# Two block products of the last projection taken as quarter products, and a division moved by one product

## The chip, the core and the metric

The kernel runs on one core of a Trainium2 chip. The core has a matrix engine (TensorE, PE in the profile; its weight loads are shown apart as PEld), three engines for elementwise work (VectorE = DVE, ScalarE = ACT, GpSimd = POOL) and SyncE (SP), which here issues almost all DMAs. Each engine works through its own list of instructions; semaphores tie the lists together. Matmul results are accumulated in PSUM banks; everything else lies in SBUF, the on-chip memory. The metric is the device time of one execution in microseconds (us); lower is better.

## What is computed

Two layers, one after the other, on a batch of 8 images of 512 channels and 32x32 = 1024 positions, in float32. Each layer is a group norm, an attention with 8 heads of 64 channels over the 1024 positions, an output projection with a bias, and the addition of the layer's input:

```python
xn = groupnorm(x) * gn_scale + gn_bias                        # x: (8, 512, 1024)
q, k, v = split(einsum('oc,bcn->bon', qkv_w, xn) + qkv_b, 3)
attn = softmax(einsum('bhdi,bhdj->bhij', q, k) / sqrt(64), axis=-1)
out = einsum('bhij,bhdj->bhdi', attn, v)                      # back to (8, 512, 1024)
x = einsum('oc,bcn->bon', proj_w, out) + proj_b + x
```

The two layers differ in the number of groups (8 and 32) and in the weights.

## The kernel before

**Units.** The work is cut into 16 units, one for each layer and image. A unit makes v, q and k (three products of a 512x512 weight with the 512x1024 normed input), then runs the attention in 64 steps (`attention`), each with a score matmul (line 953), an exponential on ScalarE (961), a sum on VectorE (998) and a product with v (981). The projection of a unit is worked in the following unit, between k and the attention. The last unit has no follower. Behind its attention stand therefore two projections: first that of the unit before (called here the earlier projection; `project`, line 700), then its own, the last one (`project_last`, line 833).

**Fewer products by recursion.** Every 512x512 times 512x1024 product is made as a 2x2 block product by a scheme that needs 7 block products in place of 8 (numbered 1 to 7, run in the order 1, 6, 2, 7, 5, 4, 3). It needs sums and differences of blocks. `Right` holds the right-hand side, the moving operand: `outer[k]` is the block for product k, and `mix(i)` makes one of the four differences on VectorE (line 221; `mix(0)` makes the block of product 5, `mix(1)` that of product 6 and reads the fourth pair of channels). One block product is 256x256 times 256x512. It can be done in two ways:

- as a *whole block product* (`steps` in `project_last`, matmuls at line 413): four matmuls of 128x512;
- as *quarter products*, by the same scheme once more: seven *parts*, each one matmul of 128x256 (line 448). `single(k, rooms, engine, kept)` (line 241) gives the four subtractions of 128x256 which that needs and enters the seven operands in `inner[k]`.

**The stream.** `Stream.product` (line 415 on) issues quarter products so that the tail of one lies inside the next: part 1; then `close()`, which issues the tail of the product before it (parts 4 and 3, and its `finish`); then parts 6, 2, 7 and 5. The parts 1, 6 and 5 add up in one PSUM place, `one`. Between them ScalarE copies this running sum into the quarters of the result (`seed`, line 457: 11 after part 1, 21 after part 6, 12 after part 5, 22 after part 4), and it copies part 7 to an SBUF tile `late` (line 462), which is added on GpSimd later on (`add_late`, line 557). Part 5 may overwrite `one` only when seed 21 has read it. `finish` takes the result out of PSUM, for the most part on VectorE, and calls `hook("o", k)`, which runs what was hung on product k by `at("o", k, ...)`: at this place it enters the lists of the engines.

**What is hung on the earlier projection.** In the last unit the earlier projection carries the end of the last attention: the transposition and reduction of the row sums (`transposed`, `reduced`, at products 1 and 6), the first difference `mix(0)` (at product 2), `reciprocals` (at product 7) and, at product 3, the last of all, `divide` and two bias steps. `reciprocals` (line 1032) makes the reciprocals of the softmax sums on VectorE, stores them to DRAM (`drec`) and loads them back twice, 64 rows each, spread over the rows (`rb`). `divide` (line 1054, instruction at 1056) multiplies the last 128 channels (the fourth pair of channels, in `xn` for the last unit) by `rb` on VectorE, and `add_bias` (line 1061, instruction at 1063) adds the v bias on ScalarE in two halves.

**The last projection.** `project_last` makes all seven products as whole block products, in the order 1, 5, 6, 7, 2, 4, 3. Product 1 is begun with two matmuls ahead of the tail of the earlier projection. Its result goes to an SBUF tile `p1` with the bias by two activations on ScalarE (line 866); the sums of product 5 are added to two of the four result tiles `res` (in the space of q) on VectorE (line 872); GpSimd adds `p1`, `u2` and `u3` to the result tiles (`more`, line 853); VectorE finishes them, and SyncE stores them (line 858 and on). Here the PSUM places are named outright: `sbank[1]`, `apair[0]`, `sbank[0]`, `apair[1]` in turn.

Of the kernel before, what the change touches and what calls it, by code (L numbers as in the profile page):

```python
# [13 lines left out]
AF = mybir.ActivationFunctionType  # L14
ALU = mybir.AluOpType
# [8 lines left out]
GAMMA, BETA, QB, KB, VB, PB = range(6)  # L24
# [10 lines left out]
def fast_path(ctx, tc, x, qkv_wT, proj_wT, vecs, groups, out, flag):  # L35
# [5 lines left out]
    nc = tc.nc  # L41
# [7 lines left out]
    FD2 = FD // 2  # L49
# [7 lines left out]
    def pool(name, bufs, **kw):  # L57
# [53 lines left out]
    def raw(inst):  # L111
        return getattr(inst, "ins", inst)
# [7 lines left out]
    def follows(inst, other, reason):  # L120
        tc.add_manual_dep(raw(inst), name_of(other), DEP, reason=reason)
# [21 lines left out]
    def block_rows(t, r, h):  # L143
        return t[2 * r * P : 2 * (r + 1) * P, ts(h, FD)].rearrange("(i p) n -> p i n", p=P)
# [32 lines left out]
    def mix_left(left, engine=None):  # L177

        engine = engine or nc.vector
        add, sub = engine.tensor_add, engine.tensor_sub  # L180
        f = {k: left.block[:, k - 1, :] for k in range(1, 8)}
        a11, a21, a12, a22 = (left.block[:, :, i : i + P] for i in range(0, FD, P))
        s1, s2, s4 = (left.made[:, :, i : i + P] for i in range(0, 3 * P, P))
        return [
            partial(add, f[5], f[7], f[4]), partial(sub, f[6], f[5], f[1]),
            partial(sub, f[7], f[1], f[7]), partial(sub, f[3], f[2], f[6]),
        ], [
            partial(add, s1, a21, a22), partial(sub, s2, s1, a11),
            partial(sub, a21, a11, a21), partial(sub, s4, a12, s2),
        ]  # L190
# [220 lines left out]
    def run(steps):  # L411
        for step in steps:
            step()  # L413
# [135 lines left out]
    def in_two(cols):  # L549
        return cols.rearrange("p (a b) -> p a b", a=2)  # L550

    def twice(late):
        return late[:, None, :].to_broadcast([P, 2, FD2])

    def add_late(t, late):
        cols = in_two(t[:, 1, :])
        return nc.gpsimd.tensor_add(cols, cols, twice(late))  # L557
# [275 lines left out]
    def project_last(stream, w, left, again, res, rest):  # L833

        l, b = units[w.u]
        right = w.right_o
        add = nc.vector.tensor_add

        def steps(bank, k):
            return [  # L840
                partial(
                    nc.tensor.matmul, bank[:, i, :],
                    again[:, k - 1, :] if (c, i) == (0, 1) else left.outer(k)[:, c, ts(i, P)],
                    right.outer[k][:, c, :], start=c == 0, stop=c == 1, skip_group_check=True,
                )
                for i in range(2) for c in range(2)
            ]

        def sums(name):
            return accpool.tile([P, 2, FD], F32, tag="acc", name=f"{name}_last")  # L850

        def more(r, h, t, after=None):
            n = nc.gpsimd.tensor_add(res[r, h], res[r, h], t)
            if after is not None:
                follows(n, after, "one engine at a time on SBUF")

        def store(r, h):
            nc.sync.dma_start(block_rows(out[b], r, h), res[r, h])

        first = steps(sbank[1], 1)  # L860
        run(first[:2])
        stream.close()
        run(first[2:])
        p1 = sums("p1")
        for i in range(2):
            nc.scalar.activation(p1[:, i, :], sbank[1][:, i, :], AF.Identity, bias=vec[:, l, PB, i : i + 1])
        right.mix(1)
        run(steps(apair[0], 5))
        more(0, 0, p1, right.mix(3))
        for i in range(2):  # L870
            for t in (res[0, 1], res[1, 1]):
                add(t[:, i, :], apair[0][:, i, :], t[:, i, :])
        run(steps(sbank[0], 6))
        right.mix(2)
        u2 = sums("u2")
        add(u2, sbank[0], p1)
        more(0, 1, u2, rest())
        run(steps(apair[1], 7))
        u3 = sums("u3")
        for i in range(2):  # L880
            nc.vector.scalar_tensor_tensor(
                u3[:, i, :], apair[1][:, i, :], step_vec[:, l, PB, i : i + 1], u2[:, i, :], ALU.add, ALU.add
            )
        more(1, 1, u3)
        more(1, 0, u3)
        engines = mybir.EngineType
        tc.mark_branch_hint_location(
            GENERAL, "LikelyTaken", (engines.PE, engines.Activation, engines.DVE)
        )
        run(steps(sbank[1], 2))  # L890
        add(res[0, 0], sbank[1], res[0, 0])
        store(0, 0)
        store(1, 1)
        nc.tensor.matmul(apair[1][:1, 0, :1], both, ones[:, :1], start=True, stop=True)
        nc.scalar.copy(flag, apair[1][:1, 0, :1])
        run(steps(apair[0], 4))
        good = nc.values_load(flag[0:1, 0:1], min_val=0, max_val=P)
        add(res[1, 0], apair[0], res[1, 0])
        store(1, 0)

        rows, t = block_rows(out[b], 0, 1), res[0, 1]
        for step in steps(sbank[0], 3)[:2]:
            on("PE", step(), "s0", 0)  # L903
        on("DVE", add(t[:, 0, :], sbank[0][:, 0, :], t[:, 0, :]), "s0", 0)
        nc.sync.dma_start(rows[:, 0, :], t[:, 0, :])
        for h, bank in enumerate((sbank[0][:, 1], sbank[1][:, 1])):
            cols = ts(h, FD2)
            for c in range(2):
                n = nc.tensor.matmul(  # L909
                    bank[:, :FD2], left.outer(3)[:, 1, P:] if c else again[:, 2, :], right.outer[3][:, c, cols],  # L910
                    start=c == 0, stop=c == 1, skip_group_check=True,
                )
                on("PE", n, f"s{h}", 1)
            on("DVE", add(t[:, 1, cols], bank[:, :FD2], t[:, 1, cols]), f"s{h}", 1)  # L914
            nc.sync.dma_start(rows[:, 1, cols], t[:, 1, cols])
        return good

# [199 lines left out]
    first = {sel: mix_left(left) for sel, left in (("v", slot_v), ("q", slot_q), ("k", left_first_k))}  # L1117
# [11 lines left out]
    right = Right(xn, xt)  # L1129
# [13 lines left out]
    for u in range(2 * B):  # L1143
        w = Unit()
        w.u, w.right, w.last, w.ready, w.ao = u, right, {"v": []}, {}, ao
        w.v = vpool.tile([P, NT, C], F32, tag="v", name=f"v_{u}")
        l, _ = units[u]
# [3 lines left out]
        def at(sel, k, *parts):  # L1151
            hooks.setdefault((sel, k), []).extend(parts)
# [29 lines left out]
        def alone(t, row, i):  # L1182
            return t[:, row, i * FD2 : (i + 1) * FD2]

        def in_k(*which):
            return [alone(w.kp[r], row, i) for r, row, i in which]
# [96 lines left out]
        stream = Stream((u + 1) % 2)  # L1283
# [48 lines left out]
        right = Right(xn, xt) if not last else None  # L1332
        mixing = {}
        if not last:
# [5 lines left out]
            late = u == 0  # L1340
# [96 lines left out]
    both = const.tile([P, 1], F32, name="both")  # L1437
# [10 lines left out]
    at("o", 6, reduced, bias_2[1])  # L1448
    at("o", 2, partial(w.right_o.mix, 0))
    at("o", 7, reciprocals)  # L1450
    at("o", 3, divide, *bias)

    res = {(r, h): q_pairs[r][:, :, ts(h, FD)] for r in range(2) for h in range(2)}
    for (r, h), t in res.items():
# [266 lines left out]
```

## Time and profile before

| | us |
|---|---|
| median of 3 runs (3162.94 to 3163.63) | 3163.36 |
| the profiled execution, its own time | 3163.43 |
| its span, from the first to the last instruction | 3161.6 |

The mean granted clock of TensorE over the span is 0.999 of full speed. The stretches at the end (busy us of each engine, in brackets the instructions that are counted):

| stretch, us from the start | what runs | PE | DVE | ACT | POOL |
|---|---|---|---|---|---|
| 3059.0 to 3111.0 (52.0) | last half of the last attention | 52.00 (488) | 47.30 (51) | 34.45 (37) | 9.32 (9) |
| 3111.0 to 3131.4 (20.4) | earlier projection | 20.40 (98) | 18.56 (23) | 12.66 (35) | 13.35 (8) |
| 3131.4 to 3157.1 (25.7) | last projection | 25.66 (67) | 15.27 (22) | 3.55 (8) | 14.84 (7) |
| 3157.1 to 3161.6 (4.5) | last sum and stores | 0.00 | 0.42 (1) | 0.00 | 0.00 |

A float32 matmul is shown by the profile as two instructions. In the lines of the timeline each line is a group: its start, its length, the engine, the line of the kernel, the operation, output and inputs; in brackets stands the idle time ahead of it, and what ended it. In the chain of waits each line is a start, a length and what held up the end in that time.

### The profile page before, as it was taken

The numbers are of one execution on the slowest core, as the hardware profiler recorded it, in microseconds if no ns is written. First come the engines' busy times: TensorE is split into PE (matmuls) and PEld (weight loads), VectorE is DVE, ScalarE is ACT, GpSimd is POOL, SyncE is SP. The second block draws the span as 40 slices with busy tenths as digits, with TensorE's granted clock in tenths as the row PEclk, the third lists the DMA queues.
The fourth block names the chain that finished last, engine by engine and source line by source line (L and its number), as shares of the span: only waits on it lengthen the run. The fifth ranks groups of instructions, "written<-read, shape, count | busy, mean of one in ns | idle before, by whom it ended". The sixth has DMA issues, their size and how long they took to land.

```text
span 3161.6 us, 63820 instructions
## 1 busy us (share of the span) xinstructions
PE 3154.5 (100%) x24278; PEld 2030.4 (64%) x24278; DVE 2687.7 (85%) x3150; ACT 2039.9 (65%) x3573; POOL 1283.6 (41%) x982
## 2 busy tenths in 40 slices
PE   9999999999999999999999999999999999999999
PEld 8476584765847658475584756748567485674845
DVE  8988979889798897888979888798887988879787
ACT  3766767666676666766667666676666766667664
POOL 5245271542715426053361533615336162351514
PEclk9999999999999999999999999999999999999999
DMA  5333343443533324233142331423314333242302
GB/s 190 111 132 129 115 162 109 146 135 104 173 107 138 123 62 169 77 117 129 57 169 80 123 120 57 169 80 133 110 57 169 91 129 102 61 170 87 127 16 95
DMA packets 155923, 365.78 MB, mean 116 GB/s; under 512 B 30176, under 2 KB 46048, under 8 KB 155616
## 3 DMA queue, kind: packets, MB, share of 16 engines
q1 hardware_dynamic: 155040, 361.04, 34.3%
q8 instruction: 196, 3.21, 0.4%
q14 instruction: 111, 0.91, 0.1%
q10 hardware_dynamic: 576, 0.61, 0.1%
HBM read 299.72 MB, written 59.77 MB: 114 GB/s over the span
## 4 chain that ended last, share of the span: by engine, by line
PE 100%; DVE 0%; DMA 0%; ACT 0%; issue 0%; ACTq 0%
PE a L981 28%; PE s L953 27%; PE s L448 24%; PE a L448 18%; PE a L953 1%; PE a L413 1%; PE s L413 1%; PE s L348 0%; DMA xn<-x_dram 0%; DVE stats L273 0%; PE a L285 0%; PE s L909 0%; PE s L903 0%; PE s L285 0%; DVE q L914 0%
## 5 line engine op out<-in xcount | busy, mean ns | idle before, releaser
L961 ACT ACTIVATE p<-s 128x1024 f32<-128x1024 f32 x976 | 997.2, 1023 | 516.2 <-PE s L953 492.2
L981 PE MATMUL a<-p,v 64*64 64x512 f32 x8192 | 1101.0, 589 | 0.0
L953 PE MATMUL s<-q,k 64*64 64x512 f32 x7808 | 1059.2, 590 | 0.1
L998 DVE TENSOR_TENSOR acc<-acc,p 128x1024 f32<-128x1024 f32 x768 | 955.6, 1244 | 75.0 <-ACT p L961 31.6
L457 ACT COPY a<-s 128x256 f32<-128x256 f32 x1728 | 615.4, 358 | 346.9 <-PE s L448 247.0
L981 PEld LDWEIGHTS a<-p,v 64*64 64x64 f32 x8192 | 384.0, 131 | 495.3 <-ACT p L961 351.0
L953 PEld LDWEIGHTS s<-q,k 64*64 64x64 f32 x7808 | 385.4, 133 | 429.7 <-issue 429.2
L462 ACT COPY late<-s 128x256 f32<-128x256 f32 x432 | 161.0, 373 | 198.5 <-PE s L448 187.2
L448 PE MATMUL s<-k,w 128*128 128x256 f32 x672 | 195.0, 379 | 0.0
L998 DVE TENSOR_TENSOR acc<-p,p 128x1024 f32<-128x1024 f32 x128 | 156.0, 1219 | 10.0 <-ACT p L961 10.0
L1429 POOL TENSOR_TENSOR k<-xn 128x256 f32<-128x256 f32 x15 | 11.8, 787 | 369.3 <-PE s L953 260.5
L1013 DVE STREAM_TRANSPOSE tr<-acc 128x1024 f32<-128x1024 f32 x128 | 158.0, 1234 | 0.0
L1021 DVE TENSOR_REDUCE red<-tr 128x32 f32<-128x1024 f32 x128 | 154.1, 1204 | 0.0
L448 PE MATMUL a<-xn,w 128*128 128x256 f32 x492 | 146.4, 379 | 0.0
L448 PEld LDWEIGHTS s<-k,w 128*128 128x128 f32 x672 | 125.1, 190 | 18.0
L448 PE MATMUL a<-xt,w 128*128 128x256 f32 x456 | 135.7, 379 | 0.0
L305 POOL TENSOR_TENSOR y<-var,half 128x4 f32<-128x4 f32 (+1 forms) x17 | 19.7, 1157 | 277.2 <-DVE var L303 277.2
L557 POOL TENSOR_TENSOR q<-q,late 128x512 f32<-128x512 f32 x64 | 100.2, 1565 | 64.6 <-ACT a L457 45.5
L1008 DVE TENSOR_TENSOR ao<-a,tmp 128x512 f32<-128x512 f32 x120 | 82.4, 687 | 39.6 <-ACT tmp L1007 39.0
L448 PE MATMUL s<-xn,w 128*128 128x256 f32 x372 | 110.7, 379 | 0.0
L566 POOL TENSOR_TENSOR v<-v,late 128x512 f32<-128x512 f32 x60 | 89.8, 1496 | 48.8 <-DVE v L668 35.3
L448 PE MATMUL s<-xt,w 128*128 128x256 f32 x368 | 109.5, 379 | 0.0
(298 smaller groups left out, 5141.1 us busy)
## 6 DMA issues: line engine op xcount, KB each, us to landing
w<-iq SPq DMA_DIRECT2D x105, 448.0 KB, 3.5
w<-ik SPq DMA_DIRECT2D x105, 448.0 KB, 7.4
w<-io SPq DMA_DIRECT2D x105, 448.0 KB, 7.6
w<-iv SPq DMA_DIRECT2D x98, 448.0 KB, 3.7
rb<-drec SPq DMA_DIRECT2D x128, 256.0 KB, 3.9
res<-x_dram SPq DMA_DIRECT2D x32, 512.0 KB, 5.9
mid<-res SPq DMA_DIRECT2D x32, 512.0 KB, 2.8
xn<-mid SPq DMA_DIRECT2D x32, 512.0 KB, 3.6
```

The source lines that it names most:

```text
L448: nc.tensor.matmul(to, at, moving, start=start, stop=j != 1, skip_group_check=True),
L457: n = nc.scalar.copy(dst, one)
L462: on("ACT", nc.scalar.copy(late, seventh), s, 1)
L557: return nc.gpsimd.tensor_add(cols, cols, twice(late))
L566: return nc.gpsimd.tensor_add(cols, cols, parts)
L953: nc.tensor.matmul(bank[e * H : (e + 1) * H, j, :], w.k[pr][j * H : (j + 1) * H, t * P + e * H : t * P + (e + 1) * H], w.q[pr][j * H : (j ...
L961: exp = nc.scalar.activation(p, bank, AF.Exp, scale=SCALE)
L981: nc.tensor.matmul(banks[r][j * H : (j + 1) * H, :], w.v[rows, t, lo : lo + D], p[rows, j, :], start=(t == 0), stop=(t == NT - 1),)
L998: state["sums"].append(nc.vector.tensor_add(acc, state["first"] if t == 1 else acc, p))
L1008: i1 = nc.vector.tensor_add(w.ao[:, pr, ts(qh, FD)], banks[1], tmp)
L1013: nc.vector.transpose(tr, state["acc"].pop(c))
L1021: nc.vector.tensor_reduce(red[:, :, qh, :], state["tr"].rearrange("p j (f i) -> p j f i", i=BL), AX.X, ALU.add)
```

## The change

- Products 1 and 5 of the last projection become quarter products of the same stream that makes the earlier projection. `single` makes their operands: for product 1 four subtractions on GpSimd, put right ahead of the stream; for product 5 four subtractions on VectorE, hung on product 4 of the earlier projection behind the division. Their rooms are the eight 128x256 pieces of the first k pair.
- The division and its two bias steps are hung on product 4 of the earlier projection, where they were on product 3.
- `first` takes the result of product 1 out of PSUM (two activations on ScalarE, the late part added on GpSimd), `fifth` that of product 5 (four sums on VectorE, the late part added to two tiles on GpSimd).
- Product 6, still a whole block product, is begun with two matmuls ahead of the tail of product 5. The PSUM places of the products that follow are now taken by the stream's parity (`main`, `aux`, `other`, `spare_main`).

```diff
-        first = steps(sbank[1], 1)
-        run(first[:2])
+        def first(main, m, late):
+            for i in range(2):
+                n = nc.scalar.activation(
+                    p1[:, i, :], main[:, i, :], AF.Identity, bias=vec[:, l, PB, i : i + 1]
+                )
+                on("ACT", n, m, i)
+            add_late(p1, late)
+            more(0, 0, p1, mixed)
+
+        def fifth(main, m, late):
+            for i in range(2):
+                for t in (res[0, 1], res[1, 1]):
+                    on("DVE", add(t[:, i, :], main[:, i, :], t[:, i, :]), m, i)
+            for t in (res[0, 1], res[1, 1]):
+                add_late(t, late)
+
+
+        p1 = sums("p1")
+        stream.product(left.quarters(1), right.inner[1], False, first)
+        right.mix(1)
+        mixed = right.mix(3)
+        i = stream.n % 2
+        stream.product(left.quarters(5), right.inner[5], False, fifth)
+        (main, aux), (spare_main, other) = ((apair[j], sbank[1 - j]) for j in (i, 1 - i))
+        sixth = steps(other, 6)
+        run(sixth[:2])
         stream.close()
-        run(first[2:])
-        p1 = sums("p1")
-        for i in range(2):
-            nc.scalar.activation(p1[:, i, :], sbank[1][:, i, :], AF.Identity, bias=vec[:, l, PB, i : i + 1])
-        right.mix(1)
-        run(steps(apair[0], 5))
-        more(0, 0, p1, right.mix(3))
-        for i in range(2):
-            for t in (res[0, 1], res[1, 1]):
-                add(t[:, i, :], apair[0][:, i, :], t[:, i, :])
-        run(steps(sbank[0], 6))
+        run(sixth[2:])
         right.mix(2)
         u2 = sums("u2")
-        add(u2, sbank[0], p1)
+        add(u2, other, p1)
         more(0, 1, u2, rest())
-        run(steps(apair[1], 7))
+        run(steps(spare_main, 7))
...
-    at("o", 3, divide, *bias)
+    rooms = [alone(k_pairs[0], row, i) for row in range(2) for i in range(4)]
+    run(w.right_o.single(1, rooms[:3], nc.gpsimd, rooms[3]))
+    at("o", 4, divide, *bias, *w.right_o.single(5, rooms[4:7], nc.vector, rooms[7]))
```

What is left out renames PSUM places of the products 7, 2, 4 and 3. New line numbers: the sum of product 4 of the last projection stands at line 912 (898 before), the division at 1070, the bias at 1077, the subtractions of product 5 are shown at 1170 (the call in `hook`), the activations of `p1` at 862.

More of the change, by code (lines that the diff above doesn't have):

```diff
@@ L858, in store @@
             nc.sync.dma_start(block_rows(out[b], r, h), res[r, h])
-        first = steps(sbank[1], 1)
-        run(first[:2])
-        stream.close()
-        run(first[2:])
-        p1 = sums("p1")
-        for i in range(2):
-            nc.scalar.activation(p1[:, i, :], sbank[1][:, i, :], AF.Identity, bias=vec[:, l, PB, i : i + 1])
-        right.mix(1)
-        run(steps(apair[0], 5))
-        more(0, 0, p1, right.mix(3))
-        for i in range(2):
-            for t in (res[0, 1], res[1, 1]):
-                add(t[:, i, :], apair[0][:, i, :], t[:, i, :])
-        run(steps(sbank[0], 6))
+        def first(main, m, late):
[21 more added lines that the diff above has]
+        run(sixth[:2])
+        stream.close()
+        run(sixth[2:])
         right.mix(2)
         u2 = sums("u2")
-        add(u2, sbank[0], p1)
+        add(u2, other, p1)
         more(0, 1, u2, rest())
-        run(steps(apair[1], 7))
+        run(steps(spare_main, 7))
         u3 = sums("u3")
-        for i in range(2):
+        for r in range(2):
             nc.vector.scalar_tensor_tensor(
-                u3[:, i, :], apair[1][:, i, :], step_vec[:, l, PB, i : i + 1], u2[:, i, :], ALU.add, ALU.add
+                u3[:, r, :], spare_main[:, r, :], step_vec[:, l, PB, r : r + 1], u2[:, r, :], ALU.add, ALU.add
             )
@@ L889, in project_last @@
         )
-        run(steps(sbank[1], 2))
-        add(res[0, 0], sbank[1], res[0, 0])
+        run(steps(aux, 2))
+        add(res[0, 0], aux, res[0, 0])
         store(0, 0)
         store(1, 1)
-        nc.tensor.matmul(apair[1][:1, 0, :1], both, ones[:, :1], start=True, stop=True)
-        nc.scalar.copy(flag, apair[1][:1, 0, :1])
-        run(steps(apair[0], 4))
+        nc.tensor.matmul(spare_main[:1, 0, :1], both, ones[:, :1], start=True, stop=True)
+        nc.scalar.copy(flag, spare_main[:1, 0, :1])
+        run(steps(main, 4))
         good = nc.values_load(flag[0:1, 0:1], min_val=0, max_val=P)
-        add(res[1, 0], apair[0], res[1, 0])
+        add(res[1, 0], main, res[1, 0])
         store(1, 0)
         rows, t = block_rows(out[b], 0, 1), res[0, 1]
-        for step in steps(sbank[0], 3)[:2]:
-            on("PE", step(), "s0", 0)
-        on("DVE", add(t[:, 0, :], sbank[0][:, 0, :], t[:, 0, :]), "s0", 0)
+        for step in steps(other, 3)[:2]:
+            on("PE", step(), f"s{i}", 0)
+        on("DVE", add(t[:, 0, :], other[:, 0, :], t[:, 0, :]), f"s{i}", 0)
         nc.sync.dma_start(rows[:, 0, :], t[:, 0, :])
-        for h, bank in enumerate((sbank[0][:, 1], sbank[1][:, 1])):
-            cols = ts(h, FD2)
+        for h, bank in enumerate((other[:, 1], aux[:, 1])):
+            cols, name = ts(h, FD2), f"s{(i + h) % 2}"
             for c in range(2):
@@ L912, in project_last @@
                 )
-                on("PE", n, f"s{h}", 1)
-            on("DVE", add(t[:, 1, cols], bank[:, :FD2], t[:, 1, cols]), f"s{h}", 1)
+                on("PE", n, name, 1)
+            on("DVE", add(t[:, 1, cols], bank[:, :FD2], t[:, 1, cols]), name, 1)
             nc.sync.dma_start(rows[:, 1, cols], t[:, 1, cols])
```

## The prediction

> **What bounds the kernel now.** I read the page first: one engine fills the span.
>
> ```profile
> PE 3154.5 (100%) x24278; PEld 2030.4 (64%) x24278; DVE 2687.7 (85%) x3150; ACT 2039.9 (65%) x3573; POOL 1283.6 (41%) x982
> ...
> PE 100%; DVE 0%; DMA 0%; ACT 0%; issue 0%; ACTq 0%
> ```
>
> So time is won only by taking matmuls away, and lost by any instruction that makes TensorE (PE) wait. The change touches the last 50 us, so next I read the chain of waits there (start, length, what):
>
> ```profile
> 3130.71 0.86 PE s L448 x4
> 3131.57 1.72 PE s L413 x4
> ...
> 3135.87 3.43 PE a L413 x8
> 3139.30 3.69 PE s L413 x8
> ```
>
> A part of a quarter product (L448) takes 0.43 us; a 128x512 step of a whole block product (L413) 0.86 us, four of them 3.43 us. The sixth product took 3.69: 0.26 us of waiting, for the chain division, bias, mix. In all, PE waits for nothing else from 3128 on, and the last product ends at 3157.07. The timeline shows what stands around it (start, length, engine and line, output and inputs; in brackets the wait ahead):
>
> ```profile
> 3128.53 1.12 SPq L1049 DMA_DIRECT2D rb<-drec  x2
> ...
> 3130.32 0.36 ACT L457 COPY a<-s 128x256 f32<-128x256 f32 x1 [0.45 <-PE s L448]
> ...
> 3131.16 2.35 POOL L723 TENSOR_TENSOR spare<-spare,u_o 128x1024 f32<-128x1024 f32 x1
> ...
> 3135.39 1.22 DVE L1056 SCALAR_TENSOR_TENSOR xn<-xn,rb 128x1024 f32<-128x1024 f32 x1
> ...
> 3136.65 1.33 ACT L1063 ACTIVATE xn<-xn,vec 128x512 f32<-128x512 f32 x2 [2.48 <-DVE xn L1056]
> 3137.89 1.24 ACT L866 ACTIVATE p_last<-s,vec 128x512 f32<-128x512 f32 x2
> ```
>
> Two things are to be seen. The division (L1056) needs `rb`, whose two loads were only issued at 3128.53 and 3129.06. And the copy at 3130.32 is the seed that an L448 matmul at 3130.98 (part 5 of the earlier projection's third product) waits for. When `rb` is there, the DMA view tells (first issue alone, then the tile's own row):
>
> ```profile
> rb<-drec SPq DMA_DIRECT2D x1, 256.0 KB, 3.5
> ...
> DMA to landing us min/median/max: 3.5/3.7/3.9
> ```
>
> The first landed at 3128.53+3.5 = 3132.0, the second at 3129.06+3.9 = 3133.0. The load needs the reciprocals (3126.54) by way of `drec` (3127.11); nothing ahead of that is moved.
>
> [...] L866's input was ready at 3135.87, but it stood behind L1063, which waited 2.48 us for the division, and began at 3137.89. [...] L557 takes 1.27 us alone and took 2.18 beside the division; the mix at 3122.06 took 2.36 in place of 1.22 behind an L723, and the next L557 then waited for it. [...] the granted clock (third figure from the right in these stretches) after the last matmul ended at 3157.07, and in the start of the kernel:
>
> ```profile
> 8.50:9.00 0.50, 0.47 (x5) 0.47 (x6) 0.15 (x2) 0.00 (x0) 0.00 (x0) 0.76 0.99 336
> 9.00:12.00 3.00, 3.00 (x15) 3.00 (x16) 2.83 (x11) 0.85 (x2) 0.71 (x1) 0.50 1.03 350
> ...
> 3159.25:3159.50 0.25, 0.00 (x0) 0.00 (x0) 0.00 (x0) 0.00 (x0) 0.00 (x0) 0.53 0.06 16
> ```
>
> The clock fell 2.2 us after the last matmul; at the start it was low for some 3.4 us of steady work.
>
> **The change part by part.**
>
> *Fewer matmuls.* Products 1 and 5 go from 4 steps of 0.86 to 7 parts of 0.43: 3.45-3.02, twice, is **-0.86 us** of PE. The sixth's wait of 0.26 goes too, since its mix is then early: **-0.26**.
>
> *Four subtractions on GpSimd ahead of the stream* (128x256, 0.73 each by the L1384 rows). They read `xn` pairs 0 and 1 and write the room of the first k pair, which the scores have left. They start when L1384 ends, 3102.9[...]. Taken in turn, the VectorE queue is about 2.5 us late at 3109; it idles 1.85 us before the copy at 3111.15 and 0.62 before L578, so the `rb` chain does not move: 0 (at most +0.5).
>
> *The division, its two bias steps and four new subtractions, at product 4 instead of 3.* No DMA among them, and nothing on SP changes place. In the instruction order of the changed kernel, VectorE has division and subtractions ahead of product 3's L719; ScalarE has the **two bias steps ahead of the seed copy of product 3** that was at 3130.32, with everything of the stream behind it. So:
> - the division could start at 3133.0[...]; it then ends near 3134.72 (3134.25 if it is not held; 3136.0 if L557 is let in first);
> - bias from 3134.75; the pair takes 1.24 to the next instruction: 3135.99; seed 0.36: 3136.35;
> - then 0.05 and a weight load of 0.19 that nothing hides: part 5 at 3136.59 in place of 3130.98: **+5.6 us** (+5.1 to +6.9). Behind this matmul stands all that PE has left. Behind the waiting division on VectorE stand the subtractions and L719, which nobody needs before PE is running again.
> The four subtractions (128x256 with SBUF inputs is in no row; between 0.34, half of the 0.68 of a 128x512 one, and the 0.43 of L914; I take 0.4) end by 3138 and their user runs near 3141: 0.
>
> *The clock.* PE is then idle for 5.4 us, from 3131.15. By the two stretches above the clock falls inside it[...]: I take **+2.1** (0 to +3.4).
>
> *Bias of p1 on ScalarE inside the stream.* After part 3 of product 1 come two activations (1.15 to the next start by L866) ahead of the seed of product 5. Count from part 5's restart in steps of 0.43: product 1's last part starts at 4.33, its data is there at 4.97, the seed runs 6.12 to 6.48, its matmul, due at 6.06, starts at 6.72: **+0.65** (0.4 to 0.8).
>
> *GpSimd's chain at the end.* New are three late additions of 1.27. Product 5's result now comes in the middle of product 6. From there: four L872 sums 2.4, wait for a late addition 0.8, mix and u2 and bounds 3.2, then three L853 of 6.97 in all: done about 13.6 us after product 5's last matmul, while the fourth product ends 12.3 after it (14.3 before, when GpSimd was 0.6 ahead). The sum L898 and its 512 KB store wait 1.3 longer. Before, the last 1 MB of stores ran at full rate from 3156 to 3159, so the end follows: **+1.15** (0.5 to 1.5).
>
> Sum: -0.86-0.26+5.6+2.1+0.65+1.15 = +8.4. The profiled execution took 3163.43 us (span 3161.6 and 1.8 around it), 0.07 above the median of the runs: 3163.4+8.4 = **3171.8 us**, +0.27%.
>
> **Rivals.** A measurement of this kernel can tell about 0.2%, 6.3 us, from no change.
> 1. *The stall without the clock.* If PE's clock does not fall, or GpSimd's chain finds room: 3163.4+8.4-2.1-0.5 = 3169.2, inside 0.2%. [...] Against: at the start, about 1 us of idling was enough. Chance 0.15.
> 2. *The other side: the change does what its words say.* One mechanism: the divided rows are ready before the stream needs ScalarE, and -0.86-0.26 is all: 3162.3, not slower. It decides at the seed copy: to be in time the bias must start by 3129.1 and the division by 3127.9. `rb` was only issued at 3128.5; so only if ScalarE's order were other than read, or the wait covered. Chance 0.05.
> 3. [...] L557, ready at 3133.46, runs before the division: 1.27 more, and a longer time at half clock, 1.3: 3174.4. Against: at 3123.3 the waiting VectorE was served first. Chance 0.08.
>
> The forecast has 0.72; its own values lie between 3169.5 and 3174. Range for 8 in 10: 3168.0 to 3174.8, from rival 1 with the short stall to rival 3. Slower by over 0.2% (above 3169.7): the forecast less 0.04 of its lower edge, and rival 3: 0.76. Within 0.2%: rivals 1 and 2, and the edge: 0.23. Faster by 6.3 us has no mechanism: 0.01.
>
> **What would show it.** Right: L1077 (bias) directly ahead of an L457 on ScalarE with a wait of several us for the division, the division waiting for DMA `rb`; PE idle about 5.4 us in front of an L448 into `s`, released by ScalarE; PEclk below 1 behind it; a second gap of 0.6 after product 1; q's sum L912 waiting for GpSimd. Wrong: a division that starts before 3132, or PE without a gap at 3131.

## The result, and the profile after

| | before | after |
|---|---|---|
| median (lowest to highest) of 10 runs each, us | 3163.43 (3162.94 to 3164.39) | 3171.01 (3170.55 to 3172.35) |
| the profiled execution, its own time | 3163.43 | 3170.57 |
| its span | 3161.6 | 3168.8 |
| end of the last matmul in it | 3157.07 | 3163.45 |

After to before is 1.0024 (95% interval 1.0016 to 1.0033): the change costs 7.6 us, a quarter of a per cent. Of the 7.2 us that the span grew, 6.4 lie before the end of the last matmul and 0.8 behind it. Four executions among the experiments below, of three kernels, were slow ones of 4335 to 11978 us; they stand in the medians, which they move by 0.2 us at most, and not in the ratios.

The chain of waits after, where before it had nothing but matmuls (start, length, what held up the end):

```profile
3129.07 4.19 DMA rb<-drec
...
3133.36 1.25 DVE xn L1070 x2
...
3135.26 0.71 ACT xn L1077
3135.97 0.28 ACT a L457
3136.24 0.04 issue
3136.29 2.08 PE s L448 x4
...
3142.79 1.26 ACT p_last L862 x2
3144.05 0.28 ACT a L457
3144.34 0.04 issue
3144.38 0.70 PE s L448 x2
```

The end is now held up by a DMA, then VectorE, then ScalarE, and only from 3136.29 by TensorE again; at 3142.79 ScalarE is in it a second time. The timeline gives the waits:

```profile
3133.36 1.23 DVE L1070 SCALAR_TENSOR_TENSOR xn<-xn,rb 128x1024 f32<-128x1024 f32 x1 [2.13 <-DMA rb<-drec]
...
3134.63 1.33 ACT L1077 ACTIVATE xn<-xn,vec 128x512 f32<-128x512 f32 x2 [4.75 <-DVE xn L1070]
3135.88 0.36 ACT L457 COPY a<-s 128x256 f32<-128x256 f32 x1
...
3136.29 1.22 PE L448 MATMUL s<-w,w 128*128 128x256 f32 x2 [5.12 <-ACT a L457]
...
3144.38 0.70 PE L448 MATMUL s<-k,w 128*128 128x256 f32 x2 [0.40 <-ACT a L457]
...
3161.06 1.22 DVE L912 TENSOR_TENSOR q<-a,q 128x1024 f32<-128x1024 f32 x1 [3.56 <-POOL q L853]
```

Read the brackets from the top: VectorE waits for `rb`, ScalarE 4.75 us for the division, TensorE 5.12 us for one copy of 0.36 us whose data had long been there. The last line is a separate matter: the sum behind the fourth product waits for GpSimd. The granted clock behind the gap (the third figure from the right):

```profile
3135.00:3136.00 1.00, 0.00 (x0) 0.00 (x0) 1.00 (x1) 1.00 (x3) 0.72 (x1) 0.86 0.77 297
3136.00:3136.50 0.50, 0.21 (x1) 0.21 (x2) 0.43 (x2) 0.50 (x2) 0.00 (x0) 0.50 0.00 0
...
3139.00:3139.50 0.50, 0.50 (x3) 0.44 (x2) 0.00 (x0) 0.19 (x1) 0.00 (x0) 0.87 0.00 0
```

The mean of 0.86 puts the fall at about 3135.7, some 4.6 us after the last matmul had ended, and the mean of 0.87 puts the return at about 3139.1. Work from 3136.29 to there ran at half speed (granted clock 0.50, 0.86 us from one part to the next in place of 0.43), 2.8 us, and lost half of that: 1.4 us.

### The profile page after: what moved, and what is told of

It is laid out like the page before. It is cut to its first block, busy times and chain, and to the rows that moved or that the text cites. A ratio compares the mean times of both kernels' runs of the same rounds, so it can differ in the third digit from the quotient of the medians.

```text
span 3168.8 us, 63874 instructions
## 1 busy us (share of the span) xinstructions
PE 3155.5 (100%) x24290; PEld 2036.4 (64%) x24290; DVE 2693.9 (85%) x3154; ACT 2043.4 (64%) x3583; POOL 1295.7 (41%) x989
## 4 chain that ended last, share of the span: by engine, by line
PE 99%; DMA 0%; DVE 0%; ACT 0%; POOL 0%; issue 0%; SPq 0%; DVEq 0%; ACTq 0%; POOLq 0%
PE a L995 28%; PE s L967 27%; PE s L448 24%; PE a L448 18%; PE a L967 1%; PE a L413 1%; PE s L413 1%; DMA xn<-x_dram 0%; DMA rb<-drec 0%; PE s L348 0%; POOL xt L723 0%; PE a L285 0%; DVE v L221 0%; PE s L923 0%; PE s L917 0%
## 5 line engine op out<-in xcount | busy, mean ns | idle before, releaser
L557 POOL TENSOR_TENSOR q<-q,late 128x512 f32<-128x512 f32 x66 | 103.6, 1571 | 66.3 <-ACT a L457 45.5
```

## Experiments

Three questions: is it ScalarE's order that makes the gap (and not the quarter products, or the late `rb` whoever waits for it); what are the clock, the second stall and the tail worth; and is a version left that is faster than before? The kernel before was run beside each; its median lay between 3163.40 and 3163.67 us, so differences of less than about 0.5 us between experiments made at different times mean little. In each of them "theory" is what the explanation above gives, and "rival" what another one would give.

| experiment | median us | to before (95% interval) |
|---|---|---|
| division alone moved | 3170.23 | 1.0022 (1.0014 to 1.0031) |
| division back at product 3 | 3170.86 | 1.0025 (1.0015 to 1.0034) |
| bias on VectorE, subtractions first | 3168.48 | 1.0016 (1.0009 to 1.0023) |
| the gap filled with matmuls | 3168.55 | 1.0017 (1.0010 to 1.0023) |
| bias on VectorE, subtractions at product 3 | 3168.47 | 1.0016 (1.0009 to 1.0023) |
| the same, division at product 3 too | 3169.19 | 1.0018 (1.0011 to 1.0024) |
| the same, p1 and an addition on VectorE | 3168.22 | 1.0013 (1.0006 to 1.0020) |
| last GpSimd addition to VectorE, early | 3171.23 | 1.0024 (1.0015 to 1.0034) |
| subtractions on GpSimd at product 2 | 3168.83 | 1.0017 (1.0010 to 1.0024) |
| subtractions on GpSimd ahead of the stream | 3164.27 | 1.0002 (0.9994 to 1.0011) |
| last GpSimd addition to VectorE, later | 3170.33 | 1.0021 (1.0013 to 1.0029) |
| p1's activations behind a seed copy | 3170.47 | 1.0022 (1.0013 to 1.0031) |

### The division alone

```diff
-    at("o", 3, divide, *bias)
+    at("o", 4, divide, *bias)
```

> The kernel before, with only the division and its two bias steps moved from product 3 to product 4; the two block products of the last projection stay as full products of 512 columns. Theory (the order of ScalarE's list): the bias steps stand ahead of the seed copy of product 3, so TensorE waits some 5.1 us at 3131, loses about 1.4 us to the lowered clock and 0.25 to a weight load that nothing hides, and saves the 0.26 wait of the sixth product: 3163.4+6.5 = 3169.9 us (3168.9 to 3170.9), with the gap in front of part 5 as long as in the changed kernel. Rival (the quarter products are what costs; moving the division is harmless, since its data arrives at the same time as before): 3163.0 to 3163.8 and no gap at 3131.

Measured: 3170.23 us, 6.8 over the kernel before, as the theory had it. The timeline of this kernel:

```profile
3135.85 1.22 PE L448 MATMUL s<-w,w 128*128 128x256 f32 x2 [5.14 <-ACT a L457]
```

The gap is as long as in the changed kernel (5.14 and 5.12 us), with both block products still whole. So moving one call by one product is enough for the gap; the quarter products have no part in it.

### The division back at product 3

```diff
-    at("o", 4, divide, *bias, *w.right_o.single(5, rooms[4:7], nc.vector, rooms[7]))
+    at("o", 4, *w.right_o.single(5, rooms[4:7], nc.vector, rooms[7]))
+    at("o", 3, divide, *bias)
```

> The changed kernel, with the division and its bias steps put back to product 3 and only the four subtractions of product 5 left at product 4. Theory (order of ScalarE's list): the bias steps now stand ahead of the seed copy of the last projection's first product by quarters, which is due near 3134; the division still ends at 3134.6, so TensorE waits about 3.2 us there, the clock falls for less or not at all (0 to 1.5), and the second stall (0.7) and the late tail (0.8) stay, against 1.1 saved: 3167.0 to 3168.5. So putting the division back should recover only about half of the loss. Rival (the moved division is the whole loss, the quarter products are a gain of 0.9 to 1.1): 3162.3 to 3163.0.

Measured: 3170.86 us, as slow as the changed kernel, and outside both expectations. TensorE waits 5.57 us for a seed copy, at 3133.6 in place of 3131.2: the bias steps stand ahead of the seeds of the last projection's first product, which before was no stream product and needed none. That much was the theory; the size was off by 2.4 us. At product 3 the division also stands behind that product's own sum, and this time the four subtractions ran ahead of both (3130.6 to 3135.2) and held them up. The next experiment shows how. The clock was outside the expectation too (0 to 1.5 us): it stayed low for 5.0 us of work behind this gap, which loses 2.5.

### The bias on VectorE

```diff
+    def bias_v(h):
+        cols = w.ao[:, CC - 1, ts(h, FD)]
+        nc.vector.tensor_scalar_add(cols, cols, vec[:, units[w.u][0], VB, CC - 1 : CC])
-    at("o", 4, divide, *bias, *w.right_o.single(5, rooms[4:7], nc.vector, rooms[7]))
+    at("o", 4, *w.right_o.single(5, rooms[4:7], nc.vector, rooms[7]))
+    at("o", 4, divide, partial(bias_v, 1), partial(bias_v, 0))
```

> The changed kernel, division at product 4 as in it, but the bias added by two VectorE instructions behind the division and not by ScalarE (and the four subtractions ahead of the division). Theory (the order of ScalarE's list is the cause, not the wait for rb): the seed copy of product 3 runs at about 3130.4 as before, and there is no gap at 3131. The division still waits until 3133.3, now with the sums of product 3 behind it on VectorE; these end near 3137 and hold a seed copy that is due about 3135, so a shorter stall of 1 to 2.5 us is left; with the tail 3164 to 3166.5. Rival (the late rb delays the end whichever engine waits for it): 3168 to 3171.

Measured: 3168.48 us, within the rival's numbers; only the trace tells the two apart. The timeline of this kernel:

```profile
3131.34 2.58 POOL L723 TENSOR_TENSOR spare<-spare,u_o 128x1024 f32<-128x1024 f32 x1
...
3131.74 3.87 DVE L1170 TENSOR_TENSOR k<-v,k 128x256 f32<-128x256 f32 x2
...
3133.88 1.45 POOL L557 TENSOR_TENSOR xt<-xt,late 128x512 f32<-128x512 f32 x1
...
3135.87 1.21 DVE L1070 SCALAR_TENSOR_TENSOR xn<-xn,rb 128x1024 f32<-128x1024 f32 x1
...
3139.64 1.22 PE L448 MATMUL s<-k,w 128*128 128x256 f32 x2 [3.58 <-ACT a L457]
```

The gap at 3131 is gone: TensorE runs through to 3136.06, with the division later than ever. That settles what made it: ScalarE's order. But a pair of subtractions that takes 0.88 us in the changed kernel took 3.87 here. The pair ran from 3131.74 to 3135.61, beside GpSimd's L723 (to 3133.92) and L557 (to 3135.33), and behind it the division started 2.5 us later than in the changed kernel. So it was these that kept it waiting, and not `rb`, as the rival has it. The prediction reckoned, as an estimate, with such a delay for the division, and not for instructions of 0.4 us. The new stall of 3.58 us is VectorE's: the sum of product 3 stands behind it all, and the seed copy waits for the sum.

### The subtractions out of the way

Two placements on VectorE behind the division, to get rid of that hold:

```diff
+    at("o", 4, divide, partial(bias_v, 1), partial(bias_v, 0))
+    at("o", 3, *w.right_o.single(5, rooms[4:7], nc.vector, rooms[7]))
```

> As the run with the bias on VectorE behind the division at product 4, but the four subtractions stand behind the sums of product 3 and no longer ahead of the division. Theory (it was the subtractions, held by GpSimd's additions over 3131 to 3135, that kept the division until 3135.9 there; ScalarE's order made the gap at 3131): the division starts at 3133.4 as in the changed kernel, the bias pair takes 0.9, the sums of product 3 end near 3136.7, 2.5 us sooner than in that run; of its 3.6 us stall about 1.1 is left[...] (1.5 saved): 3168.5-2.5-1.5 = 3164.5 us (3163.8 to 3165.3). Rival (the late division delays the end by itself, wherever its followers stand): 3167.5 to 3169.

and with both lines at product 3:

> The changed kernel with division, bias (on VectorE) and the four subtractions in this order at product 3, behind that product's own sums. Theory: nothing that the stream needs stands behind the late division on ScalarE or VectorE any more, no gap at 3131 and none at 3136; the 1.1 saved by the quarter products is then visible, against 0.7 for the activations of p1 ahead of a seed copy and 0.8 for the late tail: 3163.4-1.1+0.7+0.8 = 3163.8 us (3163.4 to 3164.4). Rival (the quarter products cost something of their own beyond these): 3165 to 3168.

Measured: 3168.47 us, as the rival had it, and 3169.19, above both expectations. The timeline of the first and then of the second:

```profile
3132.40 1.54 DVE L1070 SCALAR_TENSOR_TENSOR xn<-xn,rb 128x1024 f32<-128x1024 f32 x1 [1.85 <-DMA rb<-drec]
...
3138.76 0.67 PE L448 MATMUL s<-k,w 128*128 128x256 f32 x2 [3.52 <-DVE k L1170]
```

```profile
3135.26 1.76 DVE L1469 TENSOR_SCALAR xn<-xn,vec 128x512 f32<-128x512 f32 x2
...
3136.71 1.42 POOL L557 TENSOR_TENSOR p_last<-p_last,late 128x512 f32<-128x512 f32 x1 [0.38 <-ACT p_last L862]
3136.93 1.48 DVE L1170 TENSOR_TENSOR k<-v 128x256 f32<-128x256 f32 x1
...
3139.02 0.67 PE L448 MATMUL s<-k,w 128*128 128x256 f32 x2 [3.75 <-DVE k L1170]
```

In the first the division waits for `rb` as in the changed kernel, and yet there is no gap at 3131: a late `rb` alone doesn't make it. The releaser of the stall is now a subtraction. The 1.5 us that the theory counts as saved are the clock's loss of the run before it, taken by estimate to be gone; the clock fell here too, at 3139.48, and 1.7 us were lost. Without a gap at 3131 TensorE reaches the first part that needs one at 3135.2; in the second kernel the division ends at that moment, and bias and subtractions are still to come. So the first rival's number was right and its mechanism wrong, and the second's mechanism was right: the quarter products do have a cost of their own, four subtractions that would have to lie ahead of the late division. In the changed kernel they end at 3137.3, and it doesn't show, since TensorE stands still until 3136.3 for another reason.

A third version kept this order and took more away (p1 taken out by two VectorE instructions with its late part, one GpSimd addition to VectorE, half of the bias later):

> As the run before in this list, with the two remaining costs taken away: p1 is taken out by two VectorE instructions that also add the late part (no ScalarE activations ahead of the seed, no GpSimd addition for p1), one of GpSimd's three last additions goes to VectorE, and only the half of the bias that the next mix needs stands ahead of it. Theory: only the saved 1.1 is left: 3162.3 us (3162.0 to 3162.8), below the kernel before. Rival (VectorE, now with more to do, lets the sixth or seventh product wait): 3163.4 to 3164.5.

Measured: 3168.22 us. The timeline of this kernel:

```profile
3135.47 1.36 DVE L1473 TENSOR_SCALAR xn<-xn,vec 128x512 f32<-128x512 f32 x1
...
3136.75 0.41 DVE L1174 TENSOR_TENSOR k<-v 128x256 f32<-128x256 f32 x1
...
3137.77 0.67 PE L448 MATMUL s<-k,w 128*128 128x256 f32 x2 [2.28 <-DVE k L1174]
```

It still waits 2.28 us for the same subtraction, 1.5 less than the second kernel above. About 0.4 of that comes from the bias step taken out from ahead of them, and 1.1 from the GpSimd addition to `p1` that is gone: beside it the first subtraction took 1.48 us, here 0.41. Another 2.2 us lie behind the last matmul, from which it takes 6.71 us to the end in place of 4.53. The likely cause, not tested apart, is that VectorE is late: the first 512 KB store is issued 3.9 us before the last matmul ends, where it was 5.9 before. Neither theory nor rival had these two in it.

### The subtractions on GpSimd

```diff
+    at("o", 2, *w.right_o.single(5, rooms[4:7], nc.gpsimd, rooms[7]))
+    at("o", 3, divide, partial(bias_v, 1), partial(bias_v, 0))
```

> As the run with division and bias at product 3 (bias on VectorE), but the four subtractions of product 5 run on GpSimd from product 2 on, when their input is mixed, and no longer behind the division. Theory (the 3.5 to 3.8 us waits of the two runs at product 3 and 4 were for the second of these subtractions, which TensorE needs at 3135.2, before the division is even over): no wait for a subtraction is left and the clock does not fall; then the sixth product waits 0 to 1.5 us for its mix, which is behind division and bias, and the late tail costs 0.8: 3164.4 us (3163.5 to 3165.5). Rival (the stall of these runs is not the subtractions' but comes with the late division in any case): 3167.5 to 3169.

Measured: 3168.83 us, within the rival's numbers. The profiled execution took 3167.05, among the fastest of this kernel, and kept its clock at 1. Its timeline:

```profile
3133.36 0.67 PE L448 MATMUL s<-k,w 128*128 128x256 f32 x2 [1.17 <-ACT a L457]
...
3138.31 0.70 PE L448 MATMUL s<-k,w 128*128 128x256 f32 x2 [0.40 <-ACT a L457]
3141.33 1.98 PE L413 MATMUL s<-v,w 128*128 128x512 f32 x4 [2.32 <-DVE v L221]
```

No wait for a subtraction is left; that part of the theory holds, and the rival's mechanism doesn't. But the sixth product waits 2.32 us, where 0 to 1.5 was expected, since GpSimd has no room there either. Its additions come 2.6 us later, VectorE waits 2.54 us for one of them (the 1.17 follows from it), and beside the others the bias steps and the mix took longer: the pair of L1469 2.78 us and the mix 2.28, against 0.88 and 1.22 where GpSimd was idle. What the other executions of this kernel lost beyond this one, no trace shows.

Last, the pause that GpSimd has ahead of the stream:

```diff
+    nc.gpsimd.tensor_sub(*(w.right_o.outer[k] for k in (5, 7, 1)))
+    run(w.right_o.single(5, rooms[4:7], nc.gpsimd, rooms[7]))
-    at("o", 2, partial(w.right_o.mix, 0))
+    w.bias_0 = bias[0]
+    at("o", 3, divide, partial(bias_v, 1))
```

with p1 and the addition as in the third version, and `w.bias_0()` ahead of `right.mix(2)`.

> The first mix of the last projection and the four subtractions of product 5 on GpSimd in the pause that it has at the end of attention (3108.6 to 3117.2 in the changed kernel); the division at product 3, one half of the bias on VectorE behind it, the other on ScalarE when all copies of the stream are issued; p1 taken out on VectorE with its late part, and one of the last three GpSimd additions on VectorE. Theory (every wait seen so far came from an instruction that stood behind the late division and was needed before it): no wait of over 0.5 us is left, and the 1.1 saved on TensorE is seen: 3162.5 us (3162.0 to 3163.3). Rival (the end is now bound by VectorE's chain from the division by the mixes and p1 to the bounds, whatever stands elsewhere): 3163.8 to 3166.

Measured: 3164.27 us; 1.0002 of the kernel before (0.9994 to 1.0011), not to be told from it, and within the rival's numbers, in part by its mechanism. The timeline of this kernel:

```profile
3108.86 3.33 POOL L1470 TENSOR_TENSOR v<-xn 128x1024 f32<-128x1024 f32 x1
...
3109.91 3.36 DVE L1016 TENSOR_TENSOR acc<-acc,p 128x1024 f32<-128x1024 f32 x1
...
3115.04 0.70 PE L448 MATMUL s<-w,w 128*128 128x256 f32 x2 [0.45 <-ACT a L457]
...
3136.82 1.36 DVE L1474 TENSOR_SCALAR xn<-xn,vec 128x512 f32<-128x512 f32 x1
...
3138.22 1.22 DVE L221 TENSOR_TENSOR v<-xn,v 128x1024 f32<-128x1024 f32 x1
...
3139.49 1.99 PE L413 MATMUL s<-v,w 128*128 128x512 f32 x4 [0.66 <-DVE v L221]
```

All long waits are gone, and what is left in this execution (3165.04 us, one of the slower of this kernel) is small: VectorE's sum of 1.22 us took 3.36 beside GpSimd's mix, from which follows a stall of 0.45 us at 3115; the sixth product waits 0.66, for VectorE's chain of division, bias and mix, in which the bias step took 1.36 us in place of 0.44; and from the last matmul to the end it takes 5.07 us in place of 4.53, with VectorE's addition ahead of the sum for the second product. That makes 1.65 against the 1.1 saved. The saving itself is seen: from part 5 of the earlier projection's third product to the end of the last matmul it takes 25.93 us (3132.20 to 3158.13), 0.16 less than before (3130.98 to 3157.07), with the wait of 0.66 in it. So it is real, and too small to pay for the operands it needs. One version was not run: this one with the addition in the later place, where the tail takes 4.6 us (see below). As an estimate from these figures it would end about 0.4 us sooner, within 0.3 us of the kernel before and still not below it.

### The clock

```diff
                 it.part(7)
+                self.fill()
                 it.keep_late()
```

`fill` issues five matmuls of 128x512 in product 3 of the earlier projection.

> The changed kernel with five more matmuls of 512 columns, whose result is not used, into a free bank ahead of part 5 of product 3: about 4.3 of the 5.1 us for which TensorE waits there are filled with work. Theory (about 1.4 us of the loss is the lowered clock): the clock stays at 1, part 5 starts when it did (3136.3) and what follows takes 0.43 a part from the first: 3171.0-1.4 = 3169.6 (3169.2 to 3170.0). Rival (the clock costs nothing, other engines set the pace behind the wait): 3171.0, within 0.3.

Measured: 3168.55 us, 2.5 less than the changed kernel, so more than expected. The timeline of this kernel:

```profile
3131.06 4.45 PE L1476 MATMUL s<-xn,w 128*128 128x512 f32 x10
3136.37 0.70 PE L449 MATMUL s<-w,w 128*128 128x256 f32 x2 [0.85 <-ACT a L458]
```

Part 5 starts when it did, the clock is 1.00 throughout, and the group that took 1.22 us takes 0.70. Doing work that nobody needs makes the kernel faster; the lowered clock is a cost by itself. How large it is depends on the execution. Five traces have the same gap of 5.12 to 5.14 us, and one has 5.57. When the clock fell and came back in them is worked out from its mean in short stretches, as for the changed kernel above (us from the start):

| kernel | clock falls | TensorE restarts | clock is back | low for | lost |
|---|---|---|---|---|---|
| changed kernel | 3135.72 | 3136.29 | 3139.13 | 3.41 | 1.4 |
| last GpSimd addition to VectorE, later | 3135.19 | 3135.66 | 3138.60 | 3.41 | 1.5 |
| last GpSimd addition to VectorE, early | by 3134.00 | 3135.65 | 3139.99 | 5.99 or more | 2.2 |
| division alone moved | 3134.56 | 3135.85 | 3141.38 | 6.82 | 2.8 |
| p1's activations behind a seed copy | 3134.84 | 3135.68 | 3141.66 | 6.82 | 3.0 |
| division back at product 3 (gap 5.57) | 3137.37 | 3139.19 | 3144.20 | 6.83 | 2.5 |

Lost is half of the time from the restart to the return: 1.4 to 3.0, over the first five rows 2.2 us on the mean. In five of these traces the fall comes 3.8 to 4.7 us after the last matmul, in the sixth (clock 0.50 from 3134.00 on, where its stretches begin) at most 3.5 us after it. Once low, the clock stayed so for 3.40 to 3.42 us in two of the six and in the three traces with gaps of 3.52 to 3.75 us (with 1.5 to 1.7 lost there), for 6.82 or 6.83 us in three, and for 5.99 us or more in one. In the five traces with about 3.4 us TensorE had restarted before the fall or did so within 0.57 us of it; in the four others it stood idle for 0.84 us or more behind the fall. What sets the moment of the fall is not shown.

### The tail

```diff
-        more(1, 0, u3)
+        add(res[1, 0], res[1, 0], u3)
```

> The changed kernel, with one of GpSimd's last three additions (the sum for the fourth product's block) on VectorE; nothing else differs. Theory (GpSimd's chain of late additions makes the end 0.8 us later against TensorE): TensorE ends where it did in the changed kernel, the sum behind the fourth product no longer waits for GpSimd, and the time falls by 0.8: 3170.2 us (3169.9 to 3170.5). Rival (the last transfers set the end, whenever that sum is ready): 3171.0, within 0.3.

Measured: 3171.23 us, no gain, within the rival's numbers. In its trace L912 no longer waits for GpSimd, and from the last matmul to the end it takes 4.75 us in place of 5.35; but on VectorE the addition (2.23 us beside GpSimd) stood ahead of the sum for the second product, and the first store was issued at 3158.78, not at 3157.53; from 3160 to 3164 the DMA engines were busy throughout (share 0.99 to 1.08, 383 to 410 GB/s). At half clock this execution lost 2.2 us, 0.8 more than the profiled one of the changed kernel. That execution, at 3170.13, is the fastest of its ten, so why the median did not fall is not shown. The addition was therefore put behind that sum:

> The changed kernel with the same addition moved from GpSimd to VectorE as in the first run on the tail, but placed behind the sum for the second product's block, so that the first 512 KB store no longer waits for it. Theory (the late tail is GpSimd's third addition, and the first run on it lost its gain again because the stores then started 1.2 us later and the last 1.5 MB went out at full rate): the first store is issued at about 3157.5 as in the changed kernel, the sum behind the fourth product starts when TensorE is done with it, and from TensorE's end to the span's end it takes 4.5 us and not 5.35: 3170.2 us (3169.7 to 3170.6). Rival (the last transfers set the end in any order): 5.2 to 5.4 us from TensorE's end, 3171.0 within 0.3.

Measured: 3170.33 us, 0.7 less than the changed kernel, and 4.6 us from the last matmul to the end. The timeline of this kernel:

```profile
3159.45 1.23 DVE L912 TENSOR_TENSOR q<-a,q 128x1024 f32<-128x1024 f32 x1 [0.21 <-PE a L413]
```

L912 now waits for TensorE. The tail is GpSimd's third addition, as predicted.

### The second stall

```diff
                 it.seed(21)
+                self.behind()
+                self.behind = lambda: None
                 it.part(2)
```

`behind` holds the two activations of p1 with what follows them, which `finish` now leaves there.

> The changed kernel with the two activations that take out p1 (and what GpSimd does with it) behind the second seed copy of product 5, no longer ahead of it. Theory (the 0.67 us second stall is these two activations in ScalarE's list): the wait of 0.40 with its unhidden weight load at 3144.4 is gone, and nothing takes its place: 3170.4 us (3170.0 to 3170.8), in the trace 0.6 to 0.7 less from TensorE's restart to the sixth product. Rival (the next seed copy is then late by as much): no change, 3171.0 within 0.3.

Measured: 3170.47 us, as the theory had it, though a median 0.5 us lower would show little by itself. No wait is left in the stream after the gap. From the restart to the sixth product it took 9.68 us, against 8.79 in the changed kernel, so on the face of it longer; but here the clock stayed low for 6.0 us of it, from the fall in the first of these stretches to the return in the second:

```profile
3134.50:3135.00 0.50, 0.00 (x0) 0.00 (x0) 0.50 (x1) 0.50 (x2) 0.50 (x1) 0.84 1.03 401
...
3141.00:3142.00 1.00, 1.00 (x5) 0.86 (x4) 1.00 (x2) 0.00 (x0) 1.00 (x1) 0.67 0.00 0
```

With the losses to the clock taken off (3.0 and 1.4) it is 6.7 against 7.4: the 0.67 us stall was ScalarE's p1.

## Why the prediction was right

Its step by step sum, with the values of the profiled execution (sum over the own time: +7.1 measured, +8.4 predicted):

| step | predicted | measured | shown by |
|---|---|---|---|
| matmuls saved, two products | -0.86 | -0.82 | what is left of the sum up to TensorE's end |
| sixth product's wait | -0.26 | -0.26 | chain: 1.72 + 1.72 in place of 3.69 |
| four subtractions on GpSimd ahead of the stream | 0 | 0 | trace |
| division and bias one product sooner | +5.6 | +5.4 | trace; division alone moved |
| clock | +2.1 | +1.4 | windows; filled gap |
| p1's activations | +0.65 | +0.67 | trace; the last experiment |
| GpSimd's chain at the end | +1.15 | +0.82 | trace; addition moved |

- **The gap.** The mechanism is the one forecast, and the experiments exclude the other two that could have looked the same: it comes without the quarter products, and it goes when only the bias leaves ScalarE. No seed copy overtook the bias in any trace: in the changed kernel the copy stood behind the bias steps until 3135.88, and the part that it copies had ended at 3131.17. Of the 5.4 us, 5.12 are the wait; the other 0.25 are an estimate for the weight load that nothing hides: the first one behind the gap took 0.29 us at the clock of 0.50, where the loads before the gap took 0.19. `rb` landed at 3133.3 where 3133.0 was forecast. One part of the step did not decide: the forecast end of the division was an estimate in which it waits for the end of GpSimd's L723, 3131.16+2.35 = 3133.51. It started at 3133.36, when its data was there, and ran beside the last 0.14 us of L723 (records of neighbours on VectorE overlap by up to 0.08 us as well); it ended at 3134.59, forecast 3134.72. So an end that close owes something to luck: `rb` came 0.3 us late, and the wait for L723 that was counted on did not come.
- **The clock.** The mis-sized term of the sum for the profiled execution, 1.4 for 2.1; over the five traces with this gap the mean is 2.2. That execution, at 3170.57, is the second fastest of the ten. So 2.1 was a good mean; all five values (1.4 to 3.0) lie in the range of 0 to 3.4 that was given with it, and which of them an execution pays could not be foreseen. Value and range were the author's estimate: half of the 3.4 us for which the clock was low at the start of the kernel before (8.76 to 12.17, from its means of 0.76 in 8.50 to 9.00 and 0.65 in 12.00 to 12.25) would have given 1.7.
- **The tail.** Right in cause, 0.3 too large: GpSimd's chain ended about 1.0 us later than L912 could have begun, not 1.3. The items named in the forecast's chain add up to 13.4 us, where it goes on with 13.6; 13.4 would have given 1.1. The stores of the kernel before, in the forecast at full rate from 3156 to 3159, moved 393, 366 and 242 GB/s in these three us (DMA share 1.03, 0.96 and 0.71).
- **The free steps.** The subtractions on GpSimd made a group of three sums on VectorE take 4.87 us in place of 3.87, and the copy behind them wait 0.30 in place of 1.85; it stands where it stood, at 3111.2. VectorE was 1.6 us late there, where 2.5 had been forecast; at 2.5 this one pause would not have covered it. The four on VectorE were put at 0 because they end before TensorE comes to them. That held, but only because TensorE was standing still; without the gap it comes to them at 3135.2, and the prediction didn't say what they cost then. The experiments that took the gap away and left the subtractions on VectorE all paid for this: 2.3 to 3.8 us of waiting. As they stand in the changed kernel the quarter products cost more than they save, by the table 0.67 and 0.82 against 0.82; the kernel with the division alone moved, 0.8 us faster, agrees.
- **Rivals.** The division ran from 3133.36 and took 1.23 us, L557 from 3133.46 and took 2.26 beside it in place of 1.27, as at 3123.30 in the kernel before, where L557 took 2.25 beside the mix; the clock fell (to 0.50); the change did not win its 1.1 us.

## What to carry to other kernels

On an engine that works its list in order, as ScalarE did in these traces, a step that waits for late data must not be put ahead of a short copy that the matmul stream needs: the 0.36 us copy paid for 4.75 us of waiting, and then for the clock. When a stall is found, ask also what it hides; here the operands of the new scheme were late as well, by 3.5 us, behind a gap of 5.1. And a saving in matmuls has to be set against where its operands are made: a pair of VectorE subtractions of 0.4 us took 3.87 us beside GpSimd's additions, and the four found no place, of those tried, in which the kernel was faster than before.

## What was not expected of the hardware

- A VectorE subtraction of 128x256 (0.42 us alone) took 1.9 us on the mean of a pair while GpSimd worked at additions of 2.58 and 1.45 us, in the run with the bias on VectorE. A VectorE addition of a constant per row with a single SBUF input (L1469, 128x512) took longer as well: 0.44 us alone, 1.4 for one beside GpSimd.
- The clock did not fall at a fixed time after the last matmul: 2.2 us at the end of the kernel before, 4.6 in the changed kernel, and in the run with the subtractions and the division at product 3 it fell at 3140.2, 4.9 us after the last matmul before the gap and 1.2 us after work had started again. Around the gaps of the last two projections it fell in all traces with one of 3.5 us or more that nothing filled, and not in the two whose longest gap was 2.3 us.
- There it stayed low for 3.40 to 3.42 us in five traces, for 6.82 or 6.83 in three, and for 5.99 or more in one. So a gap of about 5.1 us cost 1.4 to 3.0 us more than itself.
